# Attention of a three-part block: which of two small transpositions VectorE does first

## The chip, the cores and the metric

The kernel runs on one core of one Trainium2 chip. The metric is the device time of one execution in microseconds. The kernel before has a median of 2309.65 us over 3 runs (2309.11 to 2311.27).

The core's engines work side by side and are ordered by semaphores alone: PE (TensorE) multiplies matrices into PSUM banks, VectorE (DVE in the profile) and ScalarE (ACT) read those banks, GpSimd (POOL) works on the on-chip memory, and SyncE (SP) issues the copies (DMA).

## The reference

The input x has 16 batches of 512 tokens with a width of 256, in float32. The block is

```python
x = x + 0.5 * ffn(layernorm(x))       # slots that attend to the tokens, experts, and back
x = x + attn(layernorm(x))
x = x + 0.5 * ffn(layernorm(x))
```

The change is in the middle line:

```python
b, s, e = x.shape                     # 16, 512, 256; H = 16 heads of 64
q = x @ Wq + bq
kv = x @ Wkv + bkv
k, v = jnp.split(kv, [H * DQK], axis=-1)
q = _rope(q.reshape(b, s, H, DQK).transpose(0, 2, 1, 3))
k = _rope(k.reshape(b, s, H, DQK).transpose(0, 2, 1, 3))
v = v.reshape(b, s, H, DV).transpose(0, 2, 1, 3)
scores = jnp.einsum('bhqd,bhkd->bhqk', q, k) * (1.0 / np.sqrt(DQK))
scores = jnp.where(causal[None, None], scores, -jnp.inf)
probs = jax.nn.softmax(scores, axis=-1)
out = jnp.einsum('bhqk,bhkd->bhqd', probs, v)
return out.transpose(0, 2, 1, 3).reshape(b, s, H * DV) @ Wo + bo
```

## The kernel before

The kernel has three stages, one for each line of the block. In the attention stage (line 889 on) the work is cut into 64 units: 16 batches by 4 groups of 4 heads (HG = 4). A unit's queries are cut into 4 tiles of 128 tokens, numbered 0 to 3. The attention is causal, so query tile i needs only keys 0 to (i + 1) x 128 - 1: tile 3 has scores of width 512, tile 2 of 384, tile 1 of 256 and tile 0 of 128.

The main loop (line 1179) is a pipeline over units, and each engine's order in it is the order in which the code is written: in this part nothing reorders the instructions of VectorE, ScalarE, GpSimd, SyncE or PE. One turn of the loop works on several units at once. In the turn numbered u:

- `sums(u, ...)` and `leave(u, ...)` finish unit u: PE multiplies the transposed weights prT with the values (p_av, line 1132), ScalarE copies the result out, PE multiplies it with the output matrix (p_ay, line 1148), and VectorE adds it to x (line 1154).
- `old` is unit u + 1: its softmax weights are scaled and transposed, and copied to prT.
- `new` is unit u + 2: its scores are made and turned into exponentials.
- `queries_keys(u + 3)` makes the rotated queries and keys of unit u + 3 (lines 971, 977, 982, 983), and `values(u + 1, ...)` the values of unit u + 1.

A score bank is read by one VectorE instruction per head and tile (line 1047): it adds the causal mask, writes the result to the buffer pr, and leaves the row's extreme in amn. "Reading a head" below means this instruction. ScalarE then takes the exponential and the row's sum (line 1051). `scaled` inverts the sums on VectorE (line 1056), and GpSimd multiplies each head's rows by them (line 1059); for small tiles it goes over the heads, and takes tile 1 before tile 0 in each: `for i in tiles` with `tiles = (1, 0)`.

PSUM has 8 banks, which all products take in turn (`ps`, line 56). Tiles 3 and 2 of the new unit take 4 banks each, one per head. p_ay, which comes next on PE, gets a bank that a head's scores held: its first half needs tile 3's first head to have been read, its second half the second head.

The weights of tiles 2 and 3 lie in one buffer (pr, first index 0), and those of tiles 1 and 0 in another (first index 1), called the small tiles here. VectorE transposes 32 x 32 blocks of them into sq (line 1074): `turn_most(j)` handles head j's part of tiles 2 and 3 (768 elements per partition, for four heads four instructions), `turn_corner` what is left of tile 3 (512), `turn_tile(1)` small tile 1 of all four heads (1024) and `turn_tile(0)` small tile 0 of all four heads (512). `move` then issues 16 copies on SyncE (line 1101), 160 KB each, which put the blocks into prT in their final places. There is one buffer for sq and one for prT. So the next unit's first transposition, `turn_most(0)` at the end of the turn (line 1271), waits until the 16 copies have read sq; on VectorE it stands in front of the reading of the small tiles of the new unit (line 1272). Behind the 16 copies SyncE issues pieces of a later batch's transposed input (`land`, line 949).

On VectorE one turn runs in this order: two `turn_most`, `turn_most(3)`, `turn_corner`, one small tile, the reading of tile 3's first head, the other small tile, the reading of tile 3's second head and of the rest of tiles 3 and 2, the additions of line 1154, the rotations of line 977, `turn_most(0)`, and the reading of the small tiles.

Of the kernel before, what the change touches and what calls it, by code (L numbers as in the profile page):

```python
# [47 lines left out]
def macaron_kernel(ctx: ExitStack, tc: tile.TileContext, a: dict, out: bass.AP):  # L48
# [840 lines left out]
    def attention(qp, wq, wk, wv, wo, cos, sin, row):  # L889
# [24 lines left out]
        def enter(b):  # L914

            hs[b] = [qp.tile([P, 2, D], F32, tag=f"rope{2 + k}", name=f"h{b}_{k}") for k in range(2)]
            for t in range(NT):
                i = (b % PB) * NT + t
                nc.scalar.activation(hs[b][t // 2][:, t % 2, :], xs[b][:, t, :], AF.Identity,
                                     bias=shifts[b // PB][:, i:i + 1], scale=rstds[b // PB][:, i:i + 1])  # L920
# [5 lines left out]
        def width(b):  # L926
            hTs[b] = qp.tile([P, NC, S], F32, tag="hT", name=f"ahT{b}", bufs=2)
            for c in range(NC):
                pt = ps(f"p_ahT{b}_{c}")
                for t in range(NT):  # L930
                    nc.tensor.transpose(pt[:, t * P:(t + 1) * P], hs[b][t // 2][:, t % 2, c * P:(c + 1) * P], ident)
                nc.scalar.copy(hTs[b][:, c, :], pt)  # L932
# [52 lines left out]
        def values(u, t0):  # L985
            b, hg = units[u]
            if t0 == 0:
                pool, tag, bufs = (ap, "v", 1) if u + 1 < nu else (qp, "hT", 2)
                vs[u] = pool.tile([P, NT, HG * DQ], F32, tag=tag, name=f"v{b}_{hg}", bufs=bufs)
            pv = ps(f"p_v{b}_{hg}_{t0}")  # L990
            for t in range(2):
                for k in range(NC):
                    nc.tensor.matmul(pv[:, t * 256:(t + 1) * 256], hTs[b][:, k, (t0 + t) * P:(t0 + t + 1) * P],  # L993
                                     wv[:, k, hg * HG * DQ:(hg + 1) * HG * DQ],
                                     start=(k == 0), stop=(k == NC - 1))
            nc.scalar.copy(vs[u][:, t0:t0 + 2, :].rearrange("p t d -> p (t d)"), pv)  # L996
# [126 lines left out]
        def sums(u, pair):  # L1123
            b, hg = units[u]
            if pair == 0:
                oTs[u] = ap.tile([P, HG // 2, S], F32, tag="oT", name=f"aoT{b}_{hg}")
            po = ps(f"p_av{b}_{hg}_{pair}")
            for t in range(NT):
                n = NT - t
                for j in range(2):  # L1130
                    head = pair * 2 + j
                    nc.tensor.matmul(  # L1132
                        po[j * DQ:(j + 1) * DQ, :].rearrange("d (a f) -> d a f", a=NSQ)[:, :, t * SQ:],
                        vs[u][:, t, head * DQ:(head + 1) * DQ],
                        prTs[u][:, :, head, first[t] * SQ:(first[t] + n) * SQ],
                        start=(t == 0), stop=(t == NT - 1))

            r = R_BV + hg * (HG // 2) + pair
            nc.scalar.activation(oTs[u][:, pair, :].rearrange("d (i a y) -> d a i y", i=NT, a=NSQ),  # L1139
                                 po.rearrange("d (a i y) -> d a i y", i=NT, a=NSQ), AF.Identity,  # L1140
                                 bias=bcol[:, r:r + 1])
# [20 lines left out]
        def queries_keys(u):  # L1162

            if u >= nu:
                return []
            q = qs[u] = Rotated(u, "q", wq, R_BQ)
            k = ks[u] = Rotated(u, "k", wk, R_BK)
            return [lambda: q.half(0), lambda: (q.half(1), q.add()), lambda: k.half(0), lambda: (k.half(1), k.add())]
# [7 lines left out]
        with tc.tile_pool(name="awayh", bufs=2, space=bass.MemoryType.DRAM) as away, \  # L1176
                tc.manual_schedule(engines={mybir.EngineType.DVE, mybir.EngineType.Activation,
                                            mybir.EngineType.Pool, mybir.EngineType.SP}):
            for u in range(-2, nu):
                new = ws[u + 2] = Weights(u + 2) if u + 2 < nu else None  # L1180
                qk = queries_keys(u + 3)
                old = ws.get(u + 1)

                fresh = units[u + 5][0] if NHG < u + 5 < nu and units[u + 5][1] == 0 else 1 if u + 3 == NHG else None

                stats = [divmod(at, NHG) for at in range(seen, min(u + 15, NB * NHG))]
                seen = max(seen, u + 15)
                left = [divmod(u - NHG - 1, NHG)] if u >= NHG + 1 else []
                if u + 2 == nu:
                    old.scaled((1, 0))  # L1190
                    values(u + 1, 0)
                    values(u + 1, 2)
                if u >= 0:
                    sums(u, 0)
                    sums(u, 1)
                if fresh:
                    enter(fresh)
                if u + 4 in trips:
                    trips[u + 4].land((0, 1))
                if u + 3 in trips:  # L1200
                    trips[u + 3].land((2, 3))
                if old and u + 2 == nu:
                    old.turn_at_once("sq", range(0, 10, 2))
                elif u == -1:
                    values(0, 0)
                    values(0, 2)
                    old.turn_at_once("prT", range(2, 10, 3))
                elif old:
                    old.scaled((1, 0), slice(0, HG // 2))
                    old.turn_most(1)  # L1210
                    old.turn_most(2)
                    old.scaled((1, 0), slice(HG // 2, HG))
                    old.turn_most(3)
                    old.turn_corner()
                    old.turn_tile(1)
                if new:
                    new.scores((3,))
                    new.scores((2,))
                    new.exps((3,), slice(0, 1))
                if old and 0 <= u < nu - 2:  # L1220
                    old.turn_tile(0)
                    old.move()
                if new:
                    new.exps((3,), slice(1, 2))
                gone = [leave(u, 0)] if u >= 0 else []
                if fresh == 1:
                    width(1)
                if u >= 0:
                    gone.append(leave(u, 2))
                if new:  # L1230
                    new.exps((3,), slice(2, HG))
                    new.exps((2,), halfway=lambda: new.scaled((3,)))
                if u == -2:
                    new.scaled((2,))
                    new.scores((1, 0))
                    new.exps((1, 0))
                    new.scaled((1, 0))
                if u + 6 in stds:
                    scales((u + 6) // (PB * NHG), stds.pop(u + 6))
                if fresh and fresh > 1:  # L1240
                    trips[u + 5] = Trip(fresh)

                if u == nu - NHG + 1:
                    for g in range(NB // PB - 1):
                        pair_rstd(g)
                if u == nu - 1:
                    for g in range(PB):
                        entered[g] = xs[g]
                        for t in range(NT):
                            i = (g % PB) * NT + t  # L1250
                            nc.vector.tensor_scalar(xs[g][:, t, :], xs[g][:, t, :], mvs[g // PB][:, i, 0:1],
                                                    rstds[g // PB][:, i:i + 1], ALU.subtract, ALU.mult)
                for one in gone:
                    one()
                if new and u > -2:
                    new.scaled((2,))
                for one in stats + left:
                    token_stats(*one)
                for one in qk:
                    one()  # L1260
                if fresh:
                    with_bias(fresh)
                if NHG < u + 7 < nu and (u + 7) % (PB * NHG) == 0:
                    stds[u + 7] = spread((u + 7) // (PB * NHG))
                if 0 <= u < nu - 2:
                    values(u + 1, 0)
                    values(u + 1, 2)
                if new and u > -2:
                    new.scores((1, 0))
                    if u + 3 < nu:  # L1270
                        new.turn_most(0)
                    new.exps((1, 0))
            token_stats(NB - 2, NT - 1)
# [55 lines left out]
```

## Time and profile before

| What | Value |
|---|---|
| runs | 2311.27, 2309.65, 2309.11 us |
| span of the profiled execution | 2307.9 us (the page gives no other time of its own; 1.8 us under the runs' median) |
| PE busy | 2253.5 us (98%) |
| VectorE busy | 1761.7 us (76%) |
| ScalarE busy | 1122.4 us (49%) |
| GpSimd busy | 1068.0 us (46%) |
| TensorE clock granted | nine tenths or more in all 40 slices |
| copies prT<-sq | 992, of 160 KB |

The attention stage with its 62 pipelined units lies between about 450 and 1900 us, mostly at 23.3 to 24 us per unit. A line of the timeline gives start, duration, engine, line, operation, output and input, number of instructions, and in brackets the idle time in front and what ended it. A group's line gives after the bar the busy time, the mean of one instruction in ns, and the idle time in front of the group with what ended most of it. A line of busy time by stretch gives the stretch, its length, the busy time (and instructions) of PE, of PE's weight loads, of VectorE, ScalarE and GpSimd, the granted clock, the DMA engines' busy share and GB/s. Start times are counted from the start of the span.

### The profile page before, as it was taken

To read this page: it belongs to the slowest core of one execution; us is meant where nothing else is said; L and a number is where in the kernel's file an instruction comes from. 1 tells how busy PE (TensorE), PEld (TensorE's weight loads), DVE (VectorE), ACT (ScalarE), POOL (GpSimd) and SP (SyncE) were. 2 spreads that over 40 slices of the span, in tenths; PEclk is the share of its full clock that TensorE was granted. 3 is DMA by queue.
4 is the path that set the end of the run, shared out by engine and by line. 5 is a ranking of instruction groups with operands and counts; after the bars stand their busy time and mean duration, and the time that the engine had idled before them with its cause. 6 is when DMAs were issued, how large, how long until landed. Compare 5 with 4: busy or idle time off the path is not lost. (4 is left out here: it accounts for less than half of the span.)

```text
span 2307.9 us, 42376 instructions
## 1 busy us (share of the span) xinstructions
PE 2253.5 (98%) x14424; PEld 1445.6 (63%) x14424; DVE 1761.7 (76%) x4678; ACT 1122.4 (49%) x3040; POOL 1068.0 (46%) x1692
## 2 busy tenths in 40 slices
PE   7999999999999999999999999999999999998999
PEld 5664588566656556566666665555666666764588
DVE  6742398889889898889898988988888875532387
ACT  6743243555454555455454545455545455542233
POOL 2210053555656566565655565656656552210043
PEclk9999999999999999999999999999999999999999
DMA  7839851145546465555555554646555553839834
GB/s 237 243 129 407 319 138 52 30 109 133 142 105 158 96 158 121 130 131 120 137 132 125 129 142 108 157 97 154 125 127 134 119 120 112 238 127 406 315 117 140
DMA packets 221888, 358.85 MB, mean 155 GB/s; under 512 B 99877, under 2 KB 159849, under 8 KB 213481
## 3 DMA queue, kind: packets, MB, share of 16 engines
q1 hardware_dynamic: 220812, 355.34, 55.9%
q8 instruction: 115, 1.88, 0.3%
q14 instruction: 101, 0.82, 0.1%
q10 hardware_dynamic: 860, 0.81, 0.1%
HBM read 156.29 MB, written 37.22 MB: 84 GB/s over the span
## 5 line engine op out<-in xcount | busy, mean ns | idle before, releaser
L1059 POOL TENSOR_SCALAR pr<-pr,ars 128x512 f32<-128x512 f32 (+3 forms) x1024 | 524.1, 532 | 577.5 <-DVE ars L1056 576.0
L1051 ACT ACTIVATE pr<-pr,amn 128x512 f32<-128x512 f32 (+3 forms) x1024 | 561.6, 550 | 257.4 <-DVE amn L1047 252.9
L1074 DVE STREAM_TRANSPOSE sq<-pr 128x768 f32<-128x768 f32 x434 | 384.6, 918 | 131.4 <-DMA prT<-sq 94.5
L1047 DVE CUSTOM_DVE_ANT_0 pr<-p_as,causal 128x512 f32<-128x512 f32 (+3 forms) x1024 | 433.9, 480 | 8.4 <-PE p_as L1029 7.5
L1029 PE MATMUL p_as<-k,q 32*128 32x512 f32 (+3 forms) x4096 | 315.3, 441 | 0.8 <-ACT aoT L1139 0.8
L996 ACT COPY v<-p_v 128x512 f32<-128x512 f32 x128 | 74.8, 586 | 451.2 <-PE p_v L993 451.2
L1132 PE MATMUL p_av<-prT,v 128*64 128x512 f32 (+3 forms) x2048 | 289.8, 435 | 4.2 <-ACT pr L1051 2.2
L1029 PEld LDWEIGHTS p_as<-k,q 32*128 32x128 f32 x4096 | 188.7, 185 | 108.9 <-issue 74.1
L1148 PE MATMUL p_ay<-wo,aoT 128*128 128x256 f32 x1024 | 240.1, 387 | 11.3 <-DVE amn L1047 9.8
L1148 PEld LDWEIGHTS p_ay<-wo,aoT 128*128 128x128 f32 x1024 | 190.3, 191 | 73.5 <-DVE amn L1047 49.2
L993 PE MATMUL p_v<-wv,ahT 128*128 128x256 f32 x1024 | 231.6, 379 | 0.7 <-DVE x L1154 0.7
L1132 PEld LDWEIGHTS p_av<-prT,v 128*64 128x64 f32 x2048 | 139.6, 137 | 147.6 <-issue 110.7
L971 PE MATMUL p_q<-ahT,wq 128*128 128x512 f32 x512 | 230.6, 593 | 0.2 <-ACT ahT L932 0.2
L971 PE MATMUL p_k<-ahT,wk 128*128 128x512 f32 x512 | 230.3, 592 | 0.0
L993 PEld LDWEIGHTS p_v<-wv,ahT 128*128 128x128 f32 x1024 | 194.5, 190 | 53.8 <-issue 22.2
L1051 ACT ACTIVATION_READ_ACCUMULATOR pr<-pr,amn 128x1 f32 x1024 | 191.6, 187 | 0.0
L971 PEld LDWEIGHTS p_k<-ahT,wk 128*128 128x128 f32 x512 | 97.3, 190 | 122.0 <-issue 106.9
L971 PEld LDWEIGHTS p_q<-ahT,wq 128*128 128x128 f32 x512 | 97.0, 190 | 95.7 <-issue 76.3
L762 POOL TENSOR_TENSOR kbd<-kT,own 128x256 f32<-128x256 f32 x32 | 19.7, 619 | 272.0 <-DVE kT L720 240.4
L815 PE MATMUL p_cy<-vw,catT 128*128 128x256 f32 x512 | 120.8, 379 | 0.0
L588 PE MATMUL p_ds<-hT,qk 128*128 128x512 f32 x256 | 116.0, 596 | 2.1 <-ACT hT L159 2.1
L403 PE MATMUL p_cq<-hT,c_Wq 128*128 128x512 f32 x256 | 115.1, 592 | 0.0
(174 smaller groups left out, 3206.8 us busy)
## 6 DMA issues: line engine op xcount, KB each, us to landing
prT<-sq SPq DMA_DIRECT2D x992, 160.0 KB
w<-in_e_W_dram SPq DMA_DIRECT2D x64, 1024.0 KB
w<-in_e_Wg_dram SPq DMA_DIRECT2D x32, 1024.0 KB
out_dram<-x SPq DMA_DIRECT2D x64, 256.0 KB
awaya<-sqa SPq DMA_DIRECT2D x25, 512.0 KB
atT<-awaya SPq DMA_DIRECT2D x100, 128.0 KB
xl<-in_attn_x_dram SPq DMA_DIRECT2D x16, 512.0 KB
xl<-out_dram SPq DMA_DIRECT2D x16, 512.0 KB
```

The costliest lines, as they stand in the source:

```text
L403: nc.tensor.matmul(pq, w["c_Wq"][:, k, c * P:(c + 1) * P], hTs[b][:, k, :], start=(k == 0), stop=(k == NC - 1))
L588: nc.tensor.matmul(psc, qk[:, k, c * P:(c + 1) * P], hT[:, k, :], start=(k == 0), stop=(k == NC - 1))
L815: nc.tensor.matmul(py[:, t * D:(t + 1) * D], atT[:, c, t * P:(t + 1) * P], vws[b][:, c, :], start=(c == 0), stop=(c == NC - 1))
L971: nc.tensor.matmul(pq, self.w[:, k, at:at + P], hTs[self.b][:, k, :], start=(k == 0), stop=(k == NC - 1))
L993: nc.tensor.matmul(pv[:, t * 256:(t + 1) * 256], hTs[b][:, k, (t0 + t) * P:(t0 + t + 1) * P], wv[:, k, hg * HG * DQ:(hg + 1) * HG * DQ], s ...
L1029: nc.tensor.matmul(banks[j][:, at:at + w], q[n][j * 32:(j + 1) * 32, i * P:(i + 1) * P], k[n][j * 32:(j + 1) * 32, :w], start=(n == 0), st ...
L1047: nc.vector.tensor_tensor_reduce(out=self.at(i, j), in0=banks[j][:, at:at + w], in1=causal[:, S - w:], scale=-1.0 / math.sqrt(DQ), scalar= ...
L1051: nc.scalar.activation(self.at(i, j), self.at(i, j), AF.Exp, bias=self.mn[:, i, j:j + 1], scale=-1.0, accum_out=self.rs[:, i, j:j + 1])
L1059: nc.gpsimd.tensor_scalar(self.at(i, j), self.at(i, j), self.rs[:, i, j:j + 1], 1.0, ALU.mult, ALU.mult)
L1074: nc.vector.transpose(view(self.sq, j * blocks * SQ + dst[0] * SQ, [(blocks * SQ, nh)] + [(s * SQ, n) for s, (_, n) in zip(dst[1:], of)] + ...
L1132: nc.tensor.matmul(po[j * DQ:(j + 1) * DQ, :].rearrange("d (a f) -> d a f", a=NSQ)[:, :, t * SQ:], vs[u][:, t, head * DQ:(head + 1) * DQ], ...
L1148: nc.tensor.matmul(py[:, t * D:(t + 1) * D], oTs[u][:, pair, (t0 + t) * P:(t0 + t + 1) * P], wo[:, hg * (HG // 2) + pair, :], start=(pair ...
```

## The change

Small tiles 1 and 0 of the older unit change places on VectorE: tile 0 is turned in front of the reading of the new unit's tile 3, first head, and tile 1 behind it. In 62 turns of the loop two transpositions swap. `move` stays behind both.

```diff
@@ -1212,13 +1212,13 @@
                     old.scaled((1, 0), slice(HG // 2, HG))
                     old.turn_most(3)
                     old.turn_corner()
-                    old.turn_tile(1)
+                    old.turn_tile(0)
                 if new:
                     new.scores((3,))
                     new.scores((2,))
                     new.exps((3,), slice(0, 1))
                 if old and 0 <= u < nu - 2:
-                    old.turn_tile(0)
+                    old.turn_tile(1)
                     old.move()
                 if new:
                     new.exps((3,), slice(1, 2))
```

## The prediction

> **What bounds the kernel now.** I read the page's totals first (PE busy 98% of the span), then the costliest groups, for what the busy engines still wait on:
>
> ```profile
> L1074 DVE STREAM_TRANSPOSE sq<-pr 128x768 f32<-128x768 f32 x434 | 384.6, 918 | 131.4 <-DMA prT<-sq 94.5
> ...
> L1148 PE MATMUL p_ay<-wo,aoT 128*128 128x256 f32 x1024 | 240.1, 387 | 11.3 <-DVE amn L1047 9.8
> ```
>
> Two waits lie near the change. PE's output products (p_ay) stand 11.3 us in all, and what releases them is VectorE's reading of a score bank (amn, line 1047). VectorE's transpositions stand 131.4 us, mostly for the copies prT<-sq: a unit's first transposition overwrites sq, so it waits until the previous unit's 16 copies have read it.
>
> Next, the timeline of one unit, on VectorE, GpSimd, PE and SyncE:
>
> ```profile
> 1032.24 0.98 DVE L1074 STREAM_TRANSPOSE sq<-pr 128x768 f32<-128x768 f32 x1 [2.17 <-DMA prT<-sq]
> ...
> 1033.25 0.42 DVE L1047 CUSTOM_DVE_ANT_0 pr<-p_as,causal 128x256 f32<-128x256 f32 x1
> ...
> 1037.73 1.62 POOL L1059 TENSOR_SCALAR pr<-pr,ars 128x256 f32<-128x256 f32 x4 [0.15 <-DVE ars L1056]
> ...
> 1038.42 1.86 DVE L1074 STREAM_TRANSPOSE sq<-pr 128x512 f32<-128x512 f32 x2
> ...
> 1040.21 0.65 DVE L1047 CUSTOM_DVE_ANT_0 pr<-p_as,causal 128x512 f32<-128x512 f32 x1
> ...
> 1040.79 0.71 DVE L1074 STREAM_TRANSPOSE sq<-pr 128x512 f32<-128x512 f32 x1
> ...
> 1040.93 0.48 PE L1148 MATMUL p_ay<-wo,aoT 128*128 128x256 f32 x1
> ...
> 1041.42 0.65 DVE L1047 CUSTOM_DVE_ANT_0 pr<-p_as,causal 128x512 f32<-128x512 f32 x1
> ...
> 1041.56 0.51 SPq L1101 DMA_DIRECT2D prT<-sq  x1
> ```
>
> The 1.86 us at 1038.42 are the corner and small tile 1; the 0.71 us at 1040.79 are small tile 0. PE starts p_ay 0.07 us behind the end of the first head's read (1040.21 + 0.65), and does so in each of the 61 units that follow the first. The copies start 0.06 us behind the end of the last transposition (1040.79 + 0.71 = 1041.50).
>
> Then the same places in a unit of 23.8 us, against the usual 23.26 us:
>
> ```profile
> 1416.60 11.01 SPq L1101 DMA_DIRECT2D prT<-sq  x16
> ...
> 1431.23 0.98 DVE L1074 STREAM_TRANSPOSE sq<-pr 128x768 f32<-128x768 f32 x1 [2.85 <-DMA prT<-sq]
> ...
> 1432.13 0.39 DVE L1047 CUSTOM_DVE_ANT_0 pr<-p_as,causal 128x256 f32<-128x256 f32 x1
> ...
> 1437.27 1.87 DVE L1074 STREAM_TRANSPOSE sq<-pr 128x512 f32<-128x512 f32 x2
> ...
> 1440.28 0.65 DVE L1047 CUSTOM_DVE_ANT_0 pr<-p_as,causal 128x512 f32<-128x512 f32 x1
> ```
>
> This is a ring: copies start at 1416.60; 14.63 us later the first transposition may start; 0.90 us later the small tiles are read; 5.77 us later small tile 1 is turned (1437.27 + 1.87 - 1.25 = 1437.90); 2.52 us later the next copies start (1437.90 + 2.52 = 1440.42). Together 23.82 us, and no wait for PE in it. Going through the timeline unit by unit, 30 of the 61 intervals are ruled by this ring: the first small read follows its transposition by the least there is, 0.90 us. In the other 31 the read is held by PE's scores, but not long: the first unit above shows 1.01 us, so 0.11 us to spare. In 22 the spare is 0.04 to 0.33 us (sum 3.3 us), in 9 it is 0.33 to 1.76 us. Ring and PE are nearly equal; whatever lengthens the ring by a third of a microsecond lengthens almost every unit.
>
> Are the copies themselves able to give? The busy time by stretch says no:
>
> ```profile
> 1019.00:1031.00 12.00, 12.00 (x42) 7.55 (x41) 10.81 (x28) 5.07 (x15) 9.01 (x12) 1.00 0.95 219
> ```
>
> The DMA engines are 95% busy at 219 GB/s; the 16 copies (16 x 160 KB = 2.6 MB) take 12 us at that rate. A later start means a later landing.
>
> **The change, part by part.** No instruction is added or removed; on VectorE two transpositions of 62 units change places, while the order on PE, ScalarE, GpSimd and SyncE stays. Durations, by form:
>
> ```profile
> L1059 POOL TENSOR_SCALAR pr<-pr,ars 128x128 f32<-128x128 f32 x244 | 90.7, 372 | 0.0
> ...
> L1074 DVE STREAM_TRANSPOSE sq<-pr 128x512 f32<-128x512 f32 x122 | 83.9, 688 | 0.0
> ...
> L1074 DVE STREAM_TRANSPOSE sq<-pr 128x1024 f32<-128x1024 f32 x61 | 76.0, 1246 | 0.0
> ```
>
> By size alone the swap puts 1.25 - 0.69 = 0.56 us less in front of the first head's read. But GpSimd scales a head's tile 1 (0.48 us) before its tile 0 (0.37 us), so tile 0 of the last head is the last of all, done at 1037.73 + 1.62 = 1039.35. Today small tile 1 needs only the scaling before that one: it is done at 1039.01 (1039.35 less 0.37 us, and scalings overlap by 0.03), and the transposition starts at 1039.04 (1038.42 + 1.86 - 1.25). Turned first, tile 0 has to wait until 1039.35 + 0.03 = 1039.38, 0.34 us of VectorE idle. In all units the last scaling ends 0.31 us behind the start of small tile 1's transposition, so this holds for each.
>
> From there: an operation follows a transposition 0.08 us before its end (1040.21 against 1040.29), so behind tile 0 (0.67 us for the corner of the same shape, 0.71 us for tile 0 today) the first read starts at 1039.97 to 1040.01, which is 0.20 to 0.24 us earlier than 1040.21. Tile 1 starts 0.58 us later, at 1040.55 to 1040.60, and ends 1.25 us on, at 1041.80 to 1041.84: 0.30 to 0.34 us later than today's 1041.50. Everything behind it moves by that: the second head's read, the copies, the reads, additions and rotations that follow. I take 0.33 us, nearer the upper end because tile 0's own row (0.71 us) is the nearest.
>
> What the 0.33 us meets:
> - *p_ay, first products.* Released 0.20 us earlier at least. How much of it PE can use: behind p_as (384 wide) p_ay's first matmul comes 0.50 us after the last one's start; at the change from p_as (128 wide) to p_av it is 0.20 us; the 256 further columns take 256 x 0.43/512 = 0.21 us (a 512-wide matmul is issued each 0.43 us). So 0.50 - 0.41 = 0.09 us is wait. This is gained only where PE rules the interval, not where the ring does; the other end is all 0.20 us.
> - *p_ay, second products.* They start 1.83 us behind the first, at 1042.56 to 1042.67; the second head's bank is free at 1041.42 + 0.65 + 0.33 + 0.07 = 1042.47. Covered by 0.09 us at least; nothing taken.
> - *The rest of VectorE's unit.* Hidden: its last rotation is followed by a wait for the copies in all 61 units (2.17 and 2.85 us above, 0.8 us at least).
> - *ScalarE and GpSimd.* The exponentials from the second head on and GpSimd's scaling of tiles 3 and 2 come 0.33 us later; GpSimd stands 5.3 us before the latter. Nothing.
> - *SyncE.* The same 16 copies, 0.33 us later, and behind them the 8 pieces of the next batch's transposed input. SyncE stands idle 565.5 us over 62 units before the copies, 9 us each; hidden.
> - *The ring.* 0.33 us longer per unit.
>
> Sum over the 61 intervals, each lengthened by 0.33 us less its spare, and never shortened by more than 0.09 us: 30 x 0.33 = 9.9; 22 x 0.33 - 3.3 = 4.0; the 9 with most to spare -0.4. Together +13.5 us. With 0.30 us it is 11.7, with 0.35 us 14.6. The profiled execution's span is 2307.9 us, 1.8 us under the median of 2309.65; I add the sum to the median: 2309.65 + 13.5 = **2323.2 us** (+0.6%).
>
> Two rules of the Trainium skill speak against this sum. "Perfetto Trace Analysis", section Optimizing Scalar/DVE Operations, says that where VectorE is not saturated but causes bubbles on other engines, smaller instructions may let work be done sooner; by it alone the smaller tile in front would close p_ay's 11.3 us, and the time would be an estimated 2298.4 us. "DMA: Bandwidth & Descriptors", section Specifications, gives a fabric ceiling of 435 GB/s; by it the 2.6 MB would take an estimated 6 us, the copies would land well ahead of need and the ring would not bind. The rows above show 219 GB/s at 95% busy, and decide.
>
> **The rivals.**
> *The later copies are hidden (not slower).* Place: the landing of the copies. For it: in 31 intervals something is to spare. Against it: in 30 nothing is, and the DMA engines are full. If the landing moved by nothing, 31 intervals would gain 0.09 us, -2.8 us: 2306.9 us; if all 61 gained the whole 0.20 us, -12 us: 2297.5 us. By the same sum a shift of 0.07 us is even, and up to 0.17 us stays within 4.6 us. I give within the bound 0.17, really faster 0.07.
> *GpSimd is no wait (the change does what its sizes say).* Then the copies would not move, and the time is that of the rival above. Against it: 0.31 us between the two ends in every unit; only an earlier reciprocal could close it, and that one is unmoved. Counted there.
> *A second stall (slower still).* The 0.09 us before p_ay's second products run out, because VectorE pays more than 0.33 us; at 0.40 us the ring's sum is 17.5, and 0.1 us more on PE in 61 units makes 23: up to 2333 us. Chance 0.06.
>
> **How the numbers follow.** Forecast 0.70, own range 2318 to 2329 (0.25 to 0.40 us, and some us for neighbouring traffic). A measurement here tells about 0.2%, 4.6 us, from no change. Slower holds the forecast and the second stall, 0.76; same 0.17; faster 0.07. For 8 in 10 the range goes down to 2310, which leaves out the faster case and some of the even one, and up to 2329, which leaves out most of the second stall.
>
> **What would show it.** In the profile after: the last scaling (line 1059) releases the transposition of small tile 0, with about 0.34 us of idle time before it; the first read starts some 0.6 us behind that transposition's start; the copies start 2.8 to 2.9 us behind where small tile 1 starts today; the wait for prT<-sq stays large, and the first small read follows its transposition by 0.90 us in nearly all units; units of 23.26 us become 23.2 to 23.6. PE's idle time before p_ay grows from 11.3 to some 25 us, since the ring is paid for there. Wrong would be: copies that take less than 13 us from start to landing when they start later, or a transposition of tile 0 that does not wait.

## The result, and the profile after

The changed kernel takes 2322.1 us (median of 4 runs, 2320.4 to 2325.6), against 2309.57 us before. The ratio is 1.0046, with a 95% interval of 1.0034 to 1.0058: slower by 12.5 us, where 13.5 us were forecast. The profiled execution has a span of 2318.7 us, 10.8 us more than before.

The two groups shown of before, on the page of the changed kernel:

```profile
L1074 DVE STREAM_TRANSPOSE sq<-pr 128x768 f32<-128x768 f32 x434 | 387.7, 918 | 149.6 <-DMA prT<-sq 105.3
...
L1148 PE MATMUL p_ay<-wo,aoT 128*128 128x256 f32 x1024 | 241.5, 389 | 18.1 <-DVE amn L1047 16.9
```

PE's idle time in front of p_ay has grown from 11.3 to 18.1 us, although the first head is read earlier. VectorE's idle time in front of the transpositions has grown from 131.4 to 149.6 us: here lie the waits for the copies and, new, the waits for GpSimd (18.3 us). The timeline of one unit, with GpSimd, VectorE, PE and SyncE:

```profile
1024.10 10.05 SPq L1101 DMA_DIRECT2D prT<-sq  x16
...
1038.05 0.98 DVE L1074 STREAM_TRANSPOSE sq<-pr 128x768 f32<-128x768 f32 x1 [2.18 <-DMA ahT<-away]
1038.95 0.38 DVE L1047 CUSTOM_DVE_ANT_0 pr<-p_as,causal 128x256 f32<-128x256 f32 x1
...
1043.39 1.63 POOL L1059 TENSOR_SCALAR pr<-pr,ars 128x256 f32<-128x256 f32 x4 [0.15 <-DVE ars L1056]
...
1045.05 0.71 DVE L1074 STREAM_TRANSPOSE sq<-pr 128x512 f32<-128x512 f32 x1 [0.30 <-POOL pr L1059]
1045.69 0.65 DVE L1047 CUSTOM_DVE_ANT_0 pr<-p_as,causal 128x512 f32<-128x512 f32 x1
...
1046.27 1.24 DVE L1074 STREAM_TRANSPOSE sq<-pr 128x1024 f32<-128x1024 f32 x1
1046.41 1.78 PE L1148 MATMUL p_ay<-wo,aoT 128*128 128x256 f32 x7 [0.22 <-DVE amn L1047]
...
1047.58 2.42 SPq L1101 DMA_DIRECT2D prT<-sq  x4
```

Three more rows of the kernel before: the copies ahead of the first unit of the prediction, and two of its unit of 23.8 us:

```profile
1018.30 10.05 SPq L1101 DMA_DIRECT2D prT<-sq  x16
...
1439.07 0.65 DVE L1047 CUSTOM_DVE_ANT_0 pr<-p_as,causal 128x512 f32<-128x512 f32 x1
...
1440.43 1.14 SPq L1101 DMA_DIRECT2D prT<-sq  x2
```

GpSimd's last scaling ends at 1043.39 + 1.63 = 1045.02, and small tile 0 starts at 1045.05 after 0.30 us of idle time. The first head is read 6.74 us behind the first small read (1045.69 - 1038.95), where it was 6.94 us in a unit that the ring ruled before (1439.07 - 1432.13). The copies start 8.63 us behind the first small read (1047.58 - 1038.95), where it was 8.30 us in that unit (1440.43 - 1432.13) and 8.29 us on the mean of the 30 intervals that the ring ruled before. So the ring has become longer by 0.34 us, and the first small read stands 0.90 us behind the start of its transposition: this unit is ruled by the ring. As what ended the transposition's wait the profile names a piece of the transposed input (ahT), which SyncE issues behind the copies; it does so for 9 transpositions here and for 10 before. The time from the copies to the transposition, 13.95 us, is that of the first unit shown of before, whose wait is put down to the copies (1032.24 - 1018.30 = 13.94). Read in the same way, 59 of the 61 intervals are now the ring's, against 30 before. From one start of the copies to the next the median is 23.55 us, against 23.27 us.

### The profile page after: what moved, and what is told of

It reads as the page before. It is cut to its first block, busy times and chain, and to the rows that moved or that the text cites. A ratio compares the mean times of both kernels' runs of the same rounds, so it can differ in the third digit from the quotient of the medians.

```text
span 2318.7 us, 42377 instructions
## 1 busy us (share of the span) xinstructions
PE 2255.0 (97%) x14424; PEld 1445.6 (62%) x14424; DVE 1761.3 (76%) x4678; ACT 1122.1 (48%) x3040; POOL 1068.1 (46%) x1692
## 5 line engine op out<-in xcount | busy, mean ns | idle before, releaser
L1074 DVE STREAM_TRANSPOSE sq<-pr 128x768 f32<-128x768 f32 x434 | 387.7, 918 | 149.6 <-DMA prT<-sq 105.3
L1148 PE MATMUL p_ay<-wo,aoT 128*128 128x256 f32 x1024 | 241.5, 389 | 18.1 <-DVE amn L1047 16.9
L1148 PEld LDWEIGHTS p_ay<-wo,aoT 128*128 128x128 f32 x1024 | 185.6, 191 | 86.2 <-DVE amn L1047 64.8
```

Of the source, the lines that this page charges most:

```text
L1074: nc.vector.transpose(view(self.sq, j * blocks * SQ + dst[0] * SQ, [(blocks * SQ, nh)] + [(s * SQ, n) for s, (_, n) in zip(dst[1:], of)] + ...
L1148: nc.tensor.matmul(py[:, t * D:(t + 1) * D], oTs[u][:, pair, (t0 + t) * P:(t0 + t + 1) * P], wo[:, hg * (HG // 2) + pair, :], start=(pair ...
```

## The experiments

Each kernel below stands beside runs of the kernel before on the same chip; their median is the time that follows "against", and the ratio is to them.

### The scaling follows: tile 0 of the last head first

```diff
 # on top of the change
             def scaled(self, tiles, heads=slice(0, HG)):
...
                 for j in range(HG)[heads]:
-                    for i in tiles:
+                    for i in tiles[::-1] if j == HG - 1 else tiles:
```

> The changed kernel, in which GpSimd scales small tile 0 of the last head before its tile 1, so that the transposition now in front has nothing to wait for. Theory (the ring through the copies): tile 0 starts where tile 1 started before, the first head is read 0.57 us earlier than before, tile 1 ends where tile 0 ended before, and the copies start within 0.05 us of before. The ring is as long as before; only the 31 intervals that PE rules gain 0.09 us: about 2307 us (2304 to 2310). Rival A (the second head's read behind the longer transposition costs PE): that read is where it was before, so also 2307 to 2310. Rival B (the longer transposition between the two reads is itself the loss, whatever GpSimd does): 2320 to 2323.

Measured: 2299.3 us (median of 5 runs) against 2312.4 us, ratio 0.9946 (0.9933 to 0.9960). The changed order on VectorE is thus a gain of 12 us as soon as GpSimd scales in the order in which VectorE reads, and this version beats both kernels. Rival B falls. But the theory's 3 us (2304 to 2310 us) were also far too few. Two groups of this kernel's page:

```profile
L1074 DVE STREAM_TRANSPOSE sq<-pr 128x768 f32<-128x768 f32 x434 | 380.3, 912 | 134.4 <-DMA prT<-sq 104.2
...
L1148 PE MATMUL p_ay<-wo,aoT 128*128 128x256 f32 x1024 | 239.0, 386 | 1.7 <-DVE amn L1047 0.9
```

VectorE waits for the copies as much as ever; 50 of 61 intervals are the ring's. But PE no longer stands before p_ay: 1.7 us, against 11.3 us. The timeline of one unit shows why:

```profile
1027.65 0.98 DVE L1074 STREAM_TRANSPOSE sq<-pr 128x768 f32<-128x768 f32 x1 [2.13 <-DMA prT<-sq]
1028.10 1.08 PE L1132 MATMUL p_av<-prT,v 128*64 128x512 f32 x4
1028.56 0.38 DVE L1047 CUSTOM_DVE_ANT_0 pr<-p_as,causal 128x256 f32<-128x256 f32 x1
...
1032.83 2.13 DVE L1074 STREAM_TRANSPOSE sq<-pr 128x768 f32<-128x768 f32 x3
1033.00 1.62 POOL L1059 TENSOR_SCALAR pr<-pr,ars 128x256 f32<-128x256 f32 x4 [0.15 <-DVE ars L1056]
...
1034.88 0.65 DVE L1047 CUSTOM_DVE_ANT_0 pr<-p_as,causal 128x512 f32<-128x512 f32 x1
1035.77 3.50 PE L1148 MATMUL p_ay<-wo,aoT 128*128 128x256 f32 x15
```

The copies made the first small read late: 0.46 us behind p_av's start, where 0.09 us is the least. Tile 0, the last of the three transpositions at 1032.83, did not wait (no idle time stands with them or with the first read), the first head's read ended at 1034.88 + 0.65 = 1035.53, and PE came for its bank 0.24 us after that, without idle time. In the kernel before, each 0.1 us of lateness was 0.1 us of standing PE, because p_ay followed the read by 0.07 us in every unit. That is the new theory: an early first read lets PE run on through a late unit, and a quick ring afterwards makes it up, so PE pays only where the ring is longer than PE's own path on the mean. Two runs below test it.

Not all of the gain is due to this. An interval is the sum of three stretches: from the copies to the transposition that awaits them, from there to the first small read (0.90 us, and any wait for PE's scores), and from there to the next copies. Over the 61 intervals of the two profiles the first stretch is 0.5 us shorter than in the kernel before, the second 6.2 us and the third 4.1 us, 10.8 us together. The third was expected to stay within 0.05 us; it is 0.07 us shorter on the mean, and 0.04 us of that is the transposition of tile 0, which takes 0.67 us right behind the corner and took 0.71 us behind a read. In the prediction's way of summing, 0.07 us off the 30 intervals of the ring and 0.09 us off the 31 of PE make 5 us. The other 6 us are what the new theory has to explain.

### The same exchange on GpSimd, under the old order on VectorE

The edit is that of the first experiment, made in the kernel before.

> The kernel before with the same exchange on GpSimd, so that small tile 1, in front there, waits 0.34 us for the last scaling. First read, second read and copies all move by about 0.33 us. Theory: both the ring and the path through PE's output products grow by it, so all 61 intervals: +17 to +21 us, 2326 to 2331. Rival A (only the second read counts): the loss of the changed kernel, 2320 to 2323.

Measured: 2332.2 us, ratio 1.0086 (1.0073 to 1.0100), +20 us, where the theory had +17 to +21 us. Small tile 1 now waits for GpSimd, and PE's idle time before p_ay is 33.3 us:

```profile
1048.73 1.25 DVE L1074 STREAM_TRANSPOSE sq<-pr 128x1024 f32<-128x1024 f32 x1 [0.29 <-POOL pr L1059]
...
L1148 PE MATMUL p_ay<-wo,aoT 128*128 128x256 f32 x1024 | 240.1, 387 | 33.3 <-DVE amn L1047 33.2
```

Order on one engine against order on the other: either mismatch costs, and the two together are the best of the four. This loss is larger than the change's own. The first read is late here as well as the copies, by 0.35 and 0.34 us on the mean, which would explain it; the two were not separated in this kernel.

### Copies later, VectorE untouched

```diff
 # on top of the kernel before, in move()
+                spare = away.tile([1, 64], F32, tag="spare", name=f"spare{self.nm}")
+                nc.sync.dma_start(spare, self.sq[0:1, 0, 0, 0:64])
                 for n in range(NSQ):
```

> The kernel before with one small copy (256 bytes of sq to memory) issued on SyncE in front of the 16: the copies start about 0.6 us later, and no instruction of VectorE, PE, ScalarE or GpSimd moves in order. Theory: the ring grows by 0.6 us; less the spare that is 30 x 0.6 + 22 x 0.6 - 3.3 + 1.6 = 29 us, 2332 to 2340. Rival A: no read is later on its own account, 2309 to 2311.

Measured: 2327.5 us, ratio 1.0074 (1.0060 to 1.0087), so +17 us, less than the 22 us at least that were expected. The timeline of this kernel, with the last transposition of a unit and SyncE, gives the reason:

```profile
1047.30 0.71 DVE L1074 STREAM_TRANSPOSE sq<-pr 128x512 f32<-128x512 f32 x1
...
1048.04 0.23 SPq L1099 DMA_DIRECT2D spare<-sq  x1
1048.36 10.04 SPq L1103 DMA_DIRECT2D prT<-sq  x16
1071.43 0.24 SPq L1099 DMA_DIRECT2D spare<-sq  x1
1071.97 3.05 SPq L1103 DMA_DIRECT2D prT<-sq  x5
```

The small copy delayed the others by 0.29 us in one unit (1048.36 less 1048.07, which is 0.06 us behind the transposition's end at 1047.30 + 0.71) and by 0.49 us in the next, not by 0.6 us; two units of the one follow two of the other, 0.37 us on the mean. With 0.37 us the prediction's own sum over the intervals gives 16 us, and the 61 intervals of the two profiles differ by 16.5 us. So a delay of the copies alone, with no read moved against the first small read, makes a loss of the kind and size of the change. The small copy adds a transfer of its own, but from the first large copy to the transposition that awaits them all the mean is 14.15 us here and 14.14 us before: its landing did not lengthen the wait.

### Second read later, copies untouched

```diff
 # on top of the kernel before
                     old.turn_tile(0)
                     old.move()
+                    spare = small.tile([P, 1], F32, tag="spare", name=f"spare{u}", bufs=1)
+                    nc.vector.tensor_reduce(spare, causal[:, 0:256], axis=AX.X, op=ALU.max)
```

> The kernel before with an idle reduction of 256 elements (about 0.3 us) on VectorE between small tile 0 and the second head's read; the copies wait for tile 0 alone and stay where they are. Theory: the second read and all that follows on VectorE come 0.3 us later and are covered by VectorE's wait for the copies (0.8 us or more): 2308 to 2312. Rival A (the second read is what costs): 2319 to 2323.

Measured: 2311.9 us against 2312.4 us, ratio 0.9997 (0.9988 to 1.0006). One unit:

```profile
1044.47 0.38 DVE L1224 TENSOR_REDUCE spare<-causal 128x1 f32<-128x256 f32 x1
1044.77 0.68 DVE L1047 CUSTOM_DVE_ANT_0 pr<-p_as,causal 128x512 f32<-128x512 f32 x1
```

The second head is read 0.3 us later (1044.77 instead of 1044.47, where the reduction begins) and everything behind it too, at no cost. Rival A falls: what costs in the change is not the read but the copies. The changed kernel's own trace agrees: p_ay's second half never starts less than 0.15 us behind the end of the second head's read, while p_ay's first half, which does wait for a read, starts 0.07 us behind it.

### A quarter fewer bytes, in both kernels and in the best version

```diff
-  nc.sync.dma_start(prT[..., q, :, :], self.sq[..., k, :, :])
+  nc.sync.dma_start(prT[..., q, 0:3, :], self.sq[..., k, 0:3, :])
...
-  prTs[u][:, :, head, first[t] * SQ:...]
+  prTs[u][:, :, min(head, 2), first[t] * SQ:...]
```

> The kernel before, whose 16 copies leave out the fourth head (a quarter of the bytes), and whose products with the values take the third head's weights for the fourth: the fourth head's result is left out, the instructions are as many and as long. Theory: the copies land some 2 us earlier, no interval is ruled by the ring, VectorE no longer waits 0.8 us and more for prT<-sq where it did, and all intervals are PE's 23.26 us with the 0.09 us before p_ay: about -11 us, 2298 to 2302. Rival A (the copies bind nothing): as before, 2309 to 2313.

> The changed kernel with the same quarter of the bytes left out (the fourth head's result is left out). Theory: without the ring the change is a gain, since only the first head's earlier read is left of it: PE's 23.17 us in all intervals, 5 to 6 us under the kernel before with fewer bytes, 2293 to 2297. Rival A (the second read costs, not the copies): 10 to 13 us over the kernel before with fewer bytes.

> The version with small tile 0 in front and scaled first, with the same quarter of the bytes left out (the fourth head's result is left out). It gained 12 us where 3 were expected. Theory now: its first head is read 0.57 us earlier, which lets PE run on when VectorE comes up to 0.5 us late, so that PE pays for the ring's mean and not for each late unit. With the ring out of the way nothing is left to be late, and it is equal to the changed kernel with fewer bytes, within 2 us: 2292 to 2297. Rival (the earlier read shortens PE's own work beyond the 0.09 us): 5 us or more under the changed kernel with fewer bytes.

| With a quarter fewer bytes | Time | Ratio to the kernel before (95%) | Median from copies to copies |
|---|---|---|---|
| kernel before | 2299.4 us | 0.9953 (0.9940 to 0.9965) | 23.26 us |
| changed kernel | 2292.8 us | 0.9925 (0.9912 to 0.9937) | 23.17 us |
| tile 0 in front and scaled first | 2289.9 us | 0.9910 (0.9895 to 0.9925) | 23.17 us |

With the ring out of the way (it rules none of the 61 intervals in the first of these kernels, and two in the second) the change turns from a loss of 12.5 us into a gain of 6.6 us; 5 to 6 us were expected. This is the strongest evidence for the ring: the change, the wait for GpSimd and the later second read are all still there, and only the copies are shorter. The pages say the same; first the kernel before with fewer bytes, then the changed one:

```profile
L1047 DVE CUSTOM_DVE_ANT_0 pr<-p_as,causal 128x512 f32<-128x512 f32 (+3 forms) x1024 | 434.9, 481 | 96.5 <-PE p_as L1029 96.5
L1074 DVE STREAM_TRANSPOSE sq<-pr 128x768 f32<-128x768 f32 x434 | 384.6, 918 | 29.9 <-DMA prT<-sq 19.9
```

```profile
L1047 DVE CUSTOM_DVE_ANT_0 pr<-p_as,causal 128x512 f32<-128x512 f32 (+3 forms) x1024 | 434.8, 480 | 70.7 <-PE p_as L1029 70.3
L1074 DVE STREAM_TRANSPOSE sq<-pr 128x768 f32<-128x768 f32 x434 | 387.5, 918 | 50.7 <-DMA prT<-sq 23.1
```

VectorE's wait has moved from the copies (94.5 us before) to PE's scores (96.5 and 70.7 us): now PE leads. In the changed kernel the second row has 21 us more in all, with only 3 us more for the copies; the difference is the wait for GpSimd, still 0.3 us per unit, and free, because VectorE would otherwise wait for PE. The best version is 2.8 us under the changed one, not within 2 us as expected, and the 95% intervals of the two overlap. The traces show where this lies: in both, 57 of the 61 intervals are 23.14 to 23.19 us, so that PE's own unit is equally long, and the rival falls. The other four are 23.11, 23.52, 24.32 and 24.63 us in the changed kernel and 22.69, 22.85, 23.47 and 24.04 us in the best version, 2.5 us less: a few units still come late, and the earlier first read makes more of that up, as the theory has it.

### An early first read, and a longer ring

```diff
 # on top of the version with tile 0 in front and scaled first
                 if old and 0 <= u < nu - 2:
+                    spare = small.tile([P, 1], F32, tag="spare", name=f"spare{u}", bufs=1)
+                    nc.vector.tensor_reduce(spare, causal[:, 0:256], axis=AX.X, op=ALU.max)
                     old.turn_tile(1)
                     old.move()
```

> The version with small tile 0 in front and scaled first, with an idle reduction of 0.3 us on VectorE between the first head's read and small tile 1: the first read stays 0.57 us earlier than before, the copies start 0.3 us later. Theory (with an early first read PE pays for the ring's mean): nearly all intervals are the ring's, whose mean grows from 23.3 to 23.6 us, +18 us over the version without the reduction: 2314 to 2320, PE idle before p_ay some 5 to 20 us. Rival (the half microsecond by which the first read is earlier absorbs a ring longer by 0.3 us for good): 2299 to 2303.

Measured: 2318.9 us (9 runs), ratio 1.0032 (1.0022 to 1.0042), within the expectation, and nearly 20 us over the version without the reduction. 60 of 61 intervals are the ring's, and their mean is 23.55 us, against 23.31 us. The early read does not absorb a ring that is longer in every unit; it only evens out units that are late now and then. The idle time before p_ay is 4.3 us on this page, just under what was expected:

```profile
L1148 PE MATMUL p_ay<-wo,aoT 128*128 128x256 f32 x1024 | 250.4, 391 | 4.3 <-DVE amn L1047 1.1
```

The busy time beside it is 11 us more than the 239.0 us of the version without the reduction. Matmul ends are modelled, so a part of PE's standing is booked as busy here, and idle time alone understates it. In this run the second head's read is late together with the copies. That alone was free in the kernel before. Here p_ay's second half follows the end of that read by 0.07 us in 47 of the 62 units, so PE now stands there too. It doesn't set the unit's length, though: in 60 of 61 intervals the first small read follows its transposition by the least there is, and so doesn't wait for PE.

## Why the prediction was right, step by step

- **The bound.** Right. The ring of copies, first transposition, small reads and next copies ruled 30 of 61 intervals and had little to spare in most others. Shortening the copies took 10 us off the kernel before (2299.4 us) and brought its units to 23.26 us, PE's own value in the prediction.
- **Small tile 0 waits for GpSimd.** Right: 0.30 us of idle time, released by line 1059, where 0.34 us was derived. Without a wait the two transpositions overlap by a few hundredths of a microsecond, which don't count as idle; counted from the first small read, the transposition's start moved by 0.33 us on the mean.
- **First read 0.20 to 0.24 us earlier, copies 0.30 to 0.34 us later, 0.33 taken.** 0.20 us; and 0.34 us against the intervals that the ring ruled before, 0.325 us on the mean of all.
- **0.09 us of wait before p_ay.** Right, and shown only by the runs with fewer bytes: 23.26 us with the wait, 23.17 us without. In the second, p_ay's first half starts 0.16 us behind the end of the first read in 56 of 62 units, not 0.07 us: the read is done 0.09 us before PE needs it.
- **The second products and the rest of VectorE's unit are covered.** Right: 0.3 us in front of the second read cost nothing in the kernel before. The 0.15 us by which p_ay's second half follows the read in the changed kernel leave 0.08 us of room, where 0.09 us was derived.
- **The sum, +13.5 us.** Measured +12.5 us by the medians and +10.8 us by the two profiled spans. Over the 61 intervals of the profiles the stretch from the first small read to the copies grew by 19.8 us, where the sum took 61 x 0.33 = 20.1; the small read's wait for PE's scores shrank by 6.6 us, as much as the sum allowed (20.1 less 13.5); and the time from the copies to the transposition that awaits them shrank by 2.7 us, where the sum had nothing. So the terms came true, and the last is why the sum is somewhat too large. Its cause is open: the mean of that time is 14.10 us against 14.14 us, but the median 14.02 us against 14.00 us, so it lies in a few units.
- **The rival "hidden".** Its price of -2.8 us counted only the intervals that PE rules. The version with tile 0 scaled first comes nearest to its condition: the copies start 0.07 us earlier instead of not at all, the first read 0.6 us earlier instead of 0.20 us. It gained 12 us, of which a sum interval by interval explains 5 us. The prediction had no term by which an early read makes up for a late unit. That its bound of -12 us (all intervals gain 0.20 us) meets the measured gain is chance, as the bound was reckoned in another way.
- **What would show it.** PE's idle time before p_ay was foreseen at some 25 us and is 18.1 us. The loss in the profiled execution is smaller than the sum, and not all of it shows there: of the 10.8 us, PE's idle time took up 9.3 us (the span less the busy time: 2318.7 - 2255.0 against 2307.9 - 2253.5), 6.8 us of them before p_ay and 2.0 us before p_av. The other signs came: the wait for GpSimd, copies 2.86 us behind the place where small tile 1 started before (counted from the first small read), and the first small read 0.90 us behind its transposition in nearly all units.
- **The rules of the Trainium skill.** "Perfetto Trace Analysis", section Optimizing Scalar/DVE Operations, speaks of breaking up instructions so that work may be completed sooner; the prediction carried this over to the order of two whole instructions, an estimated 2298.4 us with p_ay's wait closed. The change alone didn't do that (2322.1 us, and 18.1 us of idle time before p_ay). With the scaling in the same order the time was 2299.3 us, and p_ay's idle time 1.7 us, so here the smaller piece in front paid once it was no longer the last to become ready. The closeness to the estimate is in part luck, since a shorter ring and units made up add to the closed wait. The ceiling of 435 GB/s from "DMA: Bandwidth & Descriptors", section Specifications, was not what these copies reached; no run here shows it.

## What to carry to other kernels

Before putting a shorter piece of work in front, look when its input is ready: here the shorter tile was the last to be scaled, so it waited, and the longer one behind it made the copies late. The order on the engine that produces and on the engine that consumes must be changed together; each alone cost 12 to 20 us here, both together gained 12. Where two paths of nearly equal length close on each other in every unit, a hand-over without room (p_ay 0.07 us behind the read in every unit) makes the whole pay for the slower path unit by unit; half a microsecond of room there lets late units be made up, but not a path that is longer in every unit.

## What the runs showed that was not expected

- A release half a microsecond early is worth more than the wait that it removes: the wait before p_ay was 0.09 us in each of the 31 intervals that PE led, 2.8 us in all. The version with the early release gained 12 us, of which that wait and the shorter ring explain 5 us.
- A small copy of 256 bytes in front of the 16 held them up by 0.29 or 0.49 us, not by the 0.6 us that one of the large copies takes on the queue; the row of a 160 KB copy is no price for a small one.
- With the ring out of the way the period hardly varies: 57 of 61 intervals lie between 23.24 and 23.29 us in the kernel before with fewer bytes, and as many between 23.14 and 23.19 us in the changed one, so that a derived wait of 0.09 us could be checked to about a hundredth.
